# Layer one's source part by seven quarter products, one row quarter staged in pieces, and the second norm moved into layer two

## The chip, the cores and the metric

The kernel runs on one core of a Trainium2 chip. The metric is device time in microseconds (us); a comparison takes medians of several runs. TensorE (PE in the profile, PEld for its weight loads) multiplies, VectorE (DVE), ScalarE (ACT) and GpSimd (POOL) do elementwise work, and SyncE's queue (SPq) issues most DMA transfers.

## The reference, cut to what matters

For each of 16 graphs there are 1024 nodes with 128 features, `x`, and a weighted adjacency `adj` of 1024 x 1024. A first GNN is added to `x` and normalised; a second GNN of four layers, with the adjacency in both directions, is added to that and normalised again:

```python
degree = adj.sum(axis=-1)[:, :, None]
nb = einsum('bid,bij->bjd', x, adj) / degree
x = layernorm(x + relu(concat([x, nb]) @ W.T + b))

def layer(nodes):
    src_agg = einsum('bjv,bij->biv', nodes @ ws + bs, l2norm(adj, 2))   # rows normalised
    dst_agg = einsum('bjv,bji->biv', nodes @ wd + bd, l2norm(adj, 1))   # columns normalised
    self_rep = nodes @ wn + bn
    return tanh(concat([src_agg, self_rep, dst_agg]) @ wu + bu)

f1 = layer0(x); f2 = layer1(f1); f3 = layer2(concat([f2, f1]))
f4 = layer3(concat([f3, f1, x])); out = layernorm(x + f4)
```

All is in float32. The source part of a layer needs the adjacency transposed and scaled by row (`at`); the destination part needs it as it is, scaled by column (`a`).

## The kernel before, in words

One loop runs over the 16 graphs (b). For each it runs four layers, and between layer three and layer four the first GNN of the next graph (n = b + 1), whose adjacency has been loaded in the meantime. The weights `wu` are folded into the others beforehand, so that a layer is: messages (`messages`: eight node blocks times 256 columns into PSUM tiles `pt`, then VectorE adds the bias into `t`), then aggregation (`aggregate`), then tanh (`squash`).

The aggregation of a layer is a 2 x 2 block product: two halves of the features (v) by two halves of the nodes (h), with the contraction in two halves too. Where it is plain it takes 8 quarter products, four matmuls each. Winograd's form of Strassen's method takes 7: M1 to M4, Z11, Z12 and Z21, from sums of the messages (S1 to S4, made at the end of `messages`) and of the adjacency's quarters (T2 to T4 of `a`, Q2 to Q4 of `at`, made by `combine`; `combine_1` subtracts in place). The products go into six PSUM banks: Z0 and Z1 for the two node halves, and A, Bk, Ck and Dk, which share four rotating banks with the `pt` tiles. A is used for M1 and then for M3, Bk for M2, Ck for M4, Dk for the lower half of M3 (where there is one).

The matmuls are 64 columns wide, and `aggregate` issues them in pairs, one into the upper 64 partitions of PSUM (list `upper`) and one into the lower (list `lower`). One such pair is called a step below. Layers two, three and four take the seven products for both parts. Layer one of graphs 1 to 15 takes them for the destination part (DST) only, and the plain form for the source part (SRC), of which half is wanted only in the last eight steps. Layer one of graph 0 is written apart (`plain_layer`) and is not touched.

Work of the other engines is put between the steps: `events` (reads of the products, counted from the own-feature steps on) and `hooks` (by the step's number). PE, DVE, ACT and POOL run the instructions in the order of the program, which this fixes; only SyncE's order is chosen when the kernel is built, by when its transfers are expected to be ready.

The transposed adjacency `at` comes from four row quarters. Quarters 2 and 3 make `at[1]`, quarters 0 and 1 `at[0]`. Each is loaded by eight DMAs (`load_rows`), scaled by row on ACT (`scale_rows`) and transposed on VectorE (`transpose_rows`). All four are staged in parts of the old adjacency's buffer (`place`), two at a time: 2 and 3 from step 10 of layer four, 0 at step 23, 1 at step 27. The quarters 0 and 1 are transposed in layer one of the next graph, at steps 0 and 19, and the load of the adjacency after next (`load(n)`) follows the last of them.

The second norm (of the graph before) runs in layer one: `begin1` (transpose, add of the kept x, sum), `centre1`, `squares1`, `rstd1` (a power on POOL), `end1` (scaling and `store`). It works in `ys` under the tag "acc", which is also that of layer two's `e12`. Layer two runs `sums` of the next adjacency: per row block a square with its sum on ACT, a degree sum on ACT or VectorE, an add on POOL, through two buffers of the tag "sq". Layer three turns them into scale factors and scales the adjacency's columns.

Of the kernel before, what the change touches and what calls it, by code (L numbers as in the profile page):

```python
# [8 lines left out]
F32 = mybir.dt.float32  # L9
AF = mybir.ActivationFunctionType  # L10
# [13 lines left out]
def adj_resnorm_kernel(ctx: ExitStack, tc: tile.TileContext, x, adj, w0, b0, layers, out):  # L24
# [313 lines left out]
    def to_features(xs, name):  # L338

        dst = two.tile([P, N], F32, tag="xT", name=f"{name}T")  # L340
        nc.vector.transpose(dst, xs.rearrange("p k f -> p (k f)"))
        return dst
# [71 lines left out]
    def summed(name):  # L414
        return one.tile([P, K, C], F32, tag="acc", name=name)
# [30 lines left out]
    def load_rows(b, q, st, queue=nc.sync):  # L446


        v = adj[b, q * QB * C:(q + 1) * QB * C].rearrange("(k r) (h g j) -> h g r k j", r=C, h=NH, g=G)
        for g in range(G):  # L450
            for h in range(NH):
                queue.dma_start(st[g * C:(g + 1) * C, :, h * P:(h + 1) * P], v[h, g])
        return st

    def scale_rows(st, q, rinv):
        for k in range(QB):
            nc.scalar.activation(st[:, k], st[:, k], AF.Copy, scale=rinv[:, q * QB + k:q * QB + k + 1])  # L457

    def transpose_rows(st, q, at):
        h, o = divmod(q * QB * C, HW)  # L460
        for j in range(0, NB, NJ):
            nc.vector.transpose(  # L462
                at[h][:, j:j + NJ, o:o + QB * C].rearrange("p j (k c) -> p j k c", c=C),
                st.rearrange("p k (j c) -> p j k c", c=C)[:, j:j + NJ])
# [28 lines left out]
    def messages(b, l, feats, wm, between={}, with_sums=True):  # L493


        nch = CHUNKS[l]
        t = [one.tile([P, NJ, 2, 2, V], F32, tag=f"t{j}", name=f"t{l + 1}_{b}_{j}") for j in range(2)]
        for n, g in enumerate((2, 3, 0, 1)):
            pt = ps_t.tile([P, 2, 2 * P], F32, tag="pt", name=f"pt{l + 1}_{b}_{g}")
            for q in range(2):  # L500
                i = 2 * g + q
                for k, (f, c) in enumerate(feats):
                    nc.tensor.matmul(pt[:, q], f[:, i * P:(i + 1) * P], wm[:, 1 + c],  # L503
                                     start=(k == 0), stop=(k == nch - 1))
            j, o = divmod(2 * g, NJ)
            nc.vector.tensor_add(t[j][:, o:o + 2].rearrange("p k a v c -> p k (a v c)"), pt,  # L506
                                 wm[:, 0][:, None, :].to_broadcast([P, 2, 2 * P]))
            if n in between:
                between[n]()
        if not with_sums:  # L510
            return t


        s = slice(1 if l == 0 else 0, 2)
        S = {i: one.tile([P, NJ, 2, V], F32, tag=f"S{i}", name=f"S{i}_{l + 1}_{b}") for i in (2, 3, 4)}
        X = {(v, j): t[j][:, :, :, v] for v in range(2) for j in range(2)}
        S[1] = X[1, 0]
        if l == 0:
            nc.vector.tensor_sub(S[2][:, 0:2, 0], X[0, 0][:, 0:2, 0], X[1, 0][:, 0:2, 0])
        for part in (DST, SRC) if l else (DST,):  # L520
            nc.vector.tensor_sub(S[3][:, :, part], X[0, 0][:, :, part], X[1, 0][:, :, part])
        nc.vector.tensor_add(S[1][:, :, s], X[1, 0][:, :, s], X[1, 1][:, :, s])
        nc.vector.tensor_sub(S[2][:, :, s], S[1][:, :, s], X[0, 0][:, :, s])
        nc.vector.tensor_sub(S[4][:, :, s], X[0, 1][:, :, s], S[2][:, :, s])
        return X, S
# [31 lines left out]
    def aggregate(b, l, feats, msgs, a, at, T, Q, fT, etag, hooks={}, pieces=1):  # L557
# [11 lines left out]
        Dk = product(f"m3_{l}_{b}") if l else None  # L569
# [7 lines left out]

        def src(v, h, j):
            return (X[v, j // NJ][:, j % NJ, SRC], at[h][:, j])
# [30 lines left out]


        if l == 0:
            upper = [
                (Z1, True, own(1, 1)), (Z0, True, own(1, 0)),
                (Z1, False, [src(1, 1, j) for j in range(2, NB)]),
                (A, True, prod("M1", DST)), (Bk, True, prod("M2", DST)), (A, True, prod("M3", DST)),
                (Z0, False, prod("Z21", DST) + [src(1, 0, j) for j in range(NB)]),
# [3 lines left out]
                (Z1, False, [(S[2][:, j, SRC], at[1][:, j]) for j in range(2)] + [src(0, 1, j) for j in range(2, NB)]),  # L621
                (Ck, True, prod("M4", DST) + [src(1, 1, j) for j in range(2)]),
                (Z1, False, prod("Z12", DST)),
                (Z0, False, prod("Z11", DST) + [src(0, 0, j) for j in range(NB)]),
            ]
            def m4_and_m2_read():
                m4_read()
                m2_read()

            def m3_and_second_half():  # L630
                m3_read()
                second_half()

            events = {10: m1_read, 14: m4_and_m2_read, 18: m3_and_second_half}
        else:
            def m3_half():
                nc.scalar.copy(e1[high], Dk[low])

# [22 lines left out]

            def m2_and_half_of_m3():
                m2_read()
                nc.vector.tensor_add(e0[high], e0[high], e1[high])  # L664

            def last_reads():
                m3_read()
                second_half()
# [51 lines left out]
    w0n = two.tile([P, 2 * P], F32, tag="xT", name="w0n")  # L720
# [27 lines left out]
    for l, q in enumerate((2, 3, None, None)):  # L748
        fetched.append(fetch_weights(raw, l, nc.sync, None if l else wm))
        if q is not None:  # L750
            rows[q] = load_rows(0, q, places[q])
# [9 lines left out]
    xT = two.tile([P, N], F32, tag="xT", name="x0_T")  # L761
# [52 lines left out]
    x1T = two.tile([P, N], F32, tag="xT", name="x1_0_T")  # L814
# [79 lines left out]
    for q in (0, 1):  # L894
        rows[q] = load_rows(0, q, places[q], nc.gpsimd)
# [16 lines left out]
    for b in range(B):  # L912
# [4 lines left out]

# [61 lines left out]
        else:  # L979
            nm = f"1_{b - 1}"  # L980
            t = messages(b, 0, feats, wm)
            wm = message_weights(b, 1)
            w = {"ys": summed(f"y{nm}")}
            Q = combined(b, "Q")

            def begin1(w=w, nm=nm):
                transpose_rows(rows[0], 0, at)
                norm_spread(w["ys"], f4, KS)
                w["s"] = norm_sum(w["ys"], KS, nm, back)

            def scale1():
                scale_rows(rows[1], 1, rinv)

            def centre1(w=w, nm=nm):
                combine(4, y, T)
                w["sq"] = norm_centre(w["ys"], w["s"], KS, nm)

            def squares1(w=w, nm=nm):
                w["v"] = norm_squares(w["sq"], KS, nm)

            def rstd1(w=w, nm=nm):
                w["r"] = norm_rstd(w["v"], KS, nm)
                transpose_rows(rows[1], 1, at)
                if nxt:
                    w["a"] = load(n)
                    w["xs"] = load_spread(n)

            def end1(w=w):
                norm_end(w["ys"], w["r"], KS)
                store(b - 1, w["ys"], KS)  # L1010

            hooks = {0: begin1, 7: scale1, 12: centre1, 17: squares1, 19: rstd1,
                     22: lambda: combine_1(yt), 25: end1, 28: lambda: combine(2, yt, Q)}
            aggregate(b, 0, feats, t, a, at, T, Q, f1, "row", hooks)
            a2, xs2 = w.get("a"), w.get("xs")
# [7 lines left out]
        def quarters2(b=b):  # L1023
            for i in ((2, 3, 4) if b == 0 else (3, 4)):
                combine(i, yt, Q)

        hooks = {0: quarters2}
        if nxt:
            for i in ALL:
                hooks[5 + 2 * i if i < 3 else 4 + 3 * i] = lambda i=i: sums(n, a2, st, (i,))  # L1030
        if b == 0:
            hooks[12] = lambda: combine(4, y, T)
        aggregate(b, 1, feats, t, a, at, T, Q, f23, "acc", hooks)


# [43 lines left out]
        if nxt:  # L1079
# [7 lines left out]
            def add0(w=w):  # L1087
                w["ys"] = summed(f"y0_{n}")
                for h in range(NH):
                    add_x(yT, xT2, h)  # L1090
# [20 lines left out]
            def rows0():  # L1111
                for i, q in enumerate((2, 3)):
                    rows[q] = load_rows(n, q, place(i))

            def end0(w=w):
                norm_end(w["ys"], w["r"], KS)
                w["x1"] = two.tile([P, N], F32, tag="xT", name=f"x1_{n}_T")
                for h in range(NH):
                    x1_features(n, w["ys"], h, w["x1"])
                w["kept"] = put_aside(n, w["ys"])  # L1120
# [7 lines left out]
            def rows1(w=w):  # L1128
                at2[1] = transposed(n, 1)
                transpose_rows(rows[2], 2, at2)  # L1130
                scale_rows(rows[3], 3, rinv)
                w["back"] = take_back(b, kept)
                rows[0] = load_rows(n, 0, place(0))

            def rows2():
                transpose_rows(rows[3], 3, at2)
                rows[1] = load_rows(n, 1, place(1))
# [81 lines left out]
```

## Time and profile before

| | |
|---|---|
| median of three runs | 2507.22 us (2505.8 to 2507.23) |
| the profiled execution | 2505.85 us, span 2503.9 us |
| PE, PEld busy | 2484.5 us (99%), 1060.0 us (42%) |
| DVE, ACT, POOL busy | 1658.2, 836.3, 520.8 us |
| POOL power of the norms, L378 | 30 times, 5.43 us each |
| POOL add of squares, L252 | 90 times, 2.45 us each |
| row scaling, L457 | 480 times, 0.495 us each |

The span runs from the first to the last recorded instruction. A busy PE is not PE at its peak, since matmuls are pipelined and their recorded spans overlap; a length of a stage is read from the starts of its first matmuls. An L with a number is a line of the kernel before. A row of the time line has the start in us from the span's start, the length in us, engine, line, operation, output and input tiles, shape, number of merged instructions, and in brackets the idle time before it with what ended it.

### The profile page before, as it was taken

The numbers are of one execution on the slowest core, as the hardware profiler recorded it, in microseconds if no ns is written. First come the engines' busy times: TensorE is split into PE (matmuls) and PEld (weight loads), VectorE is DVE, ScalarE is ACT, GpSimd is POOL, SyncE is SP. The second block draws the span as 40 slices with busy tenths as digits, with TensorE's granted clock in tenths as the row PEclk, the third lists the DMA queues.
The fourth block names the chain that finished last, engine by engine and source line by source line (L and its number), as shares of the span: only waits on it lengthen the run. The fifth ranks groups of instructions, "written<-read, shape, count | busy, mean of one in ns | idle before, by whom it ended". The sixth has DMA issues, their size and how long they took to land.

```text
span 2503.9 us, 30302 instructions
## 1 busy us (share of the span) xinstructions
PE 2484.5 (99%) x11693; PEld 1060.0 (42%) x11693; DVE 1658.2 (66%) x2030; ACT 836.3 (33%) x1553; POOL 520.8 (21%) x217
## 2 busy tenths in 40 slices
PE   8999999999999999999999999999999999999998
PEld 4443344433444344453434434334443344433444
DVE  5858666585675757667576675766758667585643
ACT  5414333142431423324143251432414333142411
POOL 5401204112040121302113030130301203112000
PEclk9999999999999999999999999999999999999999
DMA  9418255271543615436163451635417255271410
GB/s 199 103 47 147 55 97 103 52 143 41 102 101 71 129 34 105 104 66 127 35 124 85 85 107 47 131 66 101 96 46 147 54 99 102 51 144 40 93 24 9
DMA packets 358735, 219.63 MB, mean 88 GB/s; under 512 B 148928, under 2 KB 329408, under 8 KB 358592
## 3 DMA queue, kind: packets, MB, share of 16 engines
q1 hardware_dynamic: 357184, 213.51, 42.2%
q0 software_dynamic: 1408, 4.20, 0.8%
q8 instruction: 92, 1.51, 0.3%
q14 instruction: 51, 0.42, 0.1%
HBM read 199.17 MB, written 18.46 MB: 87 GB/s over the span
## 4 chain that ended last, share of the span: by engine, by line
PE 86%; SPq 3%; DVE 2%; DMA 2%; ACT 2%; issue 2%; POOL 0%; POOLq 0%; DVEq 0%; ACTq 0%
PE m L691 34%; PE z L691 25%; PE pt L503 15%; PE pa L179 8%; SPq L231 3%; PE pw L179 2%; DMA a<-in_adj_dram 2%; DMA out_dram<-y 1%; DVE e L664 1%; ACT sq L248 0%; ACT sq L245 0%; PE d L554 0%; DVE cols L247 0%; DVE at L462 0%; POOL acc L250 0%
## 5 line engine op out<-in xcount | busy, mean ns | idle before, releaser
L378 POOL TENSOR_TENSOR rs<-ve,mhalf 128x32 f32<-128x32 f32 x30 | 162.8, 5427 | 1364.0 <-DVE ve L376 1364.0
L691 PE MATMUL m<-T,S 128*64 128x512 f32 x1008 | 395.9, 594 | 0.0
L691 PE MATMUL z<-at,t 128*64 128x512 f32 x1224 | 383.7, 592 | 0.0
L691 PE MATMUL m<-a,t 128*64 128x512 f32 x1008 | 366.8, 594 | 0.0
L691 PE MATMUL m<-Q,S 128*64 128x512 f32 x768 | 339.2, 593 | 0.0
L691 PE MATMUL m<-at,t 128*64 128x512 f32 x828 | 311.2, 592 | 0.0
L506 DVE TENSOR_TENSOR t<-pt,wm 128x512 f32<-128x512 f32 x256 | 175.4, 690 | 168.5 <-PE pt L503 168.4
L252 POOL TENSOR_TENSOR acc<-acc,sq 128x1024 f32<-128x1024 f32 x90 | 220.6, 2451 | 137.1 <-ACT sq L248 133.5
L691 PE MATMUL z<-a,S 128*64 128x512 f32 x504 | 228.3, 593 | 0.0
L691 PE MATMUL z<-a,t 128*64 128x512 f32 x504 | 226.8, 592 | 0.0
L691 PE MATMUL z<-T,t 128*64 128x512 f32 x504 | 226.8, 593 | 0.0
L336 DVE TENSOR_TENSOR a<-a,cinv 128x512 f32<-128x512 f32 x250 | 157.7, 697 | 96.3 <-DMA cinv<-dr 92.4
L457 ACT ACTIVATE a<-a,rinv 128x256 f32<-128x256 f32 x480 | 198.2, 495 | 54.9 <-DMA a<-in_adj_dram 49.5
L503 PE MATMUL pt<-wm,f1T 128*128 128x256 f32 x768 | 213.8, 384 | 0.1
L179 PE MATMUL pa<-a,xn 128*64 128x512 f32 x960 | 208.8, 592 | 0.0
L691 PE MATMUL z<-at,S 128*64 128x512 f32 x444 | 202.6, 593 | 0.0
L691 PEld LDWEIGHTS m<-Q,S 128*64 128x64 f32 x768 | 104.2, 137 | 206.6 <-issue 205.3
L591 ACT COPY e<-m 64x512 f32<-64x512 f32 x63 | 36.6, 581 | 447.8 <-PE m L691 447.5
L691 PEld LDWEIGHTS m<-T,S 128*64 128x64 f32 x1008 | 118.0, 137 | 159.6 <-issue 158.0
L691 PE MATMUL z<-Q,t 128*64 128x512 f32 x384 | 172.6, 593 | 0.0
L691 PEld LDWEIGHTS z<-at,t 128*64 128x64 f32 x1224 | 120.8, 137 | 121.0 <-issue 111.3
L691 PEld LDWEIGHTS m<-a,t 128*64 128x64 f32 x1008 | 110.1, 137 | 125.7 <-issue 120.0
(197 smaller groups left out, 3781.8 us busy)
## 6 DMA issues: line engine op xcount, KB each, us to landing
a<-in_adj_dram SPq DMA_DIRECT2D x120, 512.0 KB, 12.6
a<-in_adj_dram SPq DMA_DIRECT2D x480, 128.0 KB, 4.1
xn<-in_x_dram SPq DMA_DIRECT2D x128, 64.0 KB, 2.1
wm<-wsave SPq DMA_DIRECT2D x16, 512.0 KB, 3.9
wm<-wsave SPq DMA_DIRECT2D x31, 256.0 KB, 2.9
xs<-in_x_dram SPq DMA_DIRECT2D x60, 128.0 KB, 3.4
cinv<-dr SPq DMA_DIRECT2D x30, 256.0 KB, 5.1
dinv<-dr SPq DMA_DIRECT2D x30, 256.0 KB, 5.1
```

The source lines that it names most:

```text
L179: nc.tensor.matmul(out[s], x[:, s], y, start=start, stop=stop)
L231: nc.sync.dma_start(ov[g, :, ks], ys[g * C:(g + 1) * C, ks])
L252: nc.gpsimd.tensor_add(acc, acc, sq)
L336: engine.tensor_mul(a[:, i, s], a[:, i, s], cinv[:, s])
L378: nc.gpsimd.tensor_tensor(rstd, ve, mhalf[:, :n], ALU.pow)
L457: nc.scalar.activation(st[:, k], st[:, k], AF.Copy, scale=rinv[:, q * QB + k:q * QB + k + 1])
L503: nc.tensor.matmul(pt[:, q], f[:, i * P:(i + 1) * P], wm[:, 1 + c], start=(k == 0), stop=(k == nch - 1))
L506: nc.vector.tensor_add(t[j][:, o:o + 2].rearrange("p k a v c -> p k (a v c)"), pt, wm[:, 0][:, None, :].to_broadcast([P, 2, 2 * P]))
L591: nc.scalar.copy(e0[high], A[high])
L664: nc.vector.tensor_add(e0[high], e0[high], e1[high])
L691: nc.tensor.matmul(o, x, y, start=start, stop=stop)
```

## The change

In layer one of graphs 1 to 15 the source part is computed by the seven quarter products too. For that all of S1 to S4 are made for both parts, Dk is used, and the lists and events of layer one are new. Both row quarters of `at[0]` are transposed at step 0, T4 is made at step 3, Q2 to Q4 at steps 7, 9 and 23, and layer two no longer makes Q3 and Q4 for these graphs.

Row quarter 1 is staged in two tiles of the tag "sq" instead of the old adjacency's buffer, by 16 DMAs of half the size instead of 8; it is loaded at step 10 of layer four and scaled at step 27, before the last tanh. Quarter 0 stays where it was. The load of the next adjacency is issued at step 5 of layer one.

The second norm runs in layer two, beside the sums, with `ys` under a tag of its own ("xa"), shared with the transposed x; the transposed x1 has the tag "xb". In SyncE's queue the store of the result follows the load of the next adjacency, the weights of layer three and the load of `xs`; before, it followed the adjacency's load directly.

```diff
-        s = slice(1 if l == 0 else 0, 2)
...
-        if l == 0:
-            nc.vector.tensor_sub(S[2][:, 0:2, 0], X[0, 0][:, 0:2, 0], X[1, 0][:, 0:2, 0])
-        for part in (DST, SRC) if l else (DST,):
+        for part in (DST, SRC):
             nc.vector.tensor_sub(S[3][:, :, part], X[0, 0][:, :, part], X[1, 0][:, :, part])
-        nc.vector.tensor_add(S[1][:, :, s], X[1, 0][:, :, s], X[1, 1][:, :, s])
-        nc.vector.tensor_sub(S[2][:, :, s], S[1][:, :, s], X[0, 0][:, :, s])
-        nc.vector.tensor_sub(S[4][:, :, s], X[0, 1][:, :, s], S[2][:, :, s])
+        nc.vector.tensor_add(S[1], X[1, 0], X[1, 1])
+        nc.vector.tensor_sub(S[2], S[1], X[0, 0])
+        nc.vector.tensor_sub(S[4], X[0, 1], S[2])
...
         if l == 0:
             upper = [
                 (Z1, True, own(1, 1)), (Z0, True, own(1, 0)),
-                (Z1, False, [src(1, 1, j) for j in range(2, NB)]),
-                (A, True, prod("M1", DST)), (Bk, True, prod("M2", DST)), (A, True, prod("M3", DST)),
-                (Z0, False, prod("Z21", DST) + [src(1, 0, j) for j in range(NB)]),
+                (A, True, prod("M1", DST)), (Bk, True, prod("M2", DST)), (Z0, False, prod("Z21", DST)),
+                (A, False, prod("M1", SRC)), (Bk, False, prod("M2", SRC)), (A, True, prod("M3", SRC)),
+                (Z0, False, prod("Z21", SRC)),
             ]
             lower = [
                 (Z1, True, own(0, 1)), (Z0, True, own(0, 0)),
-                (Z1, False, [(S[2][:, j, SRC], at[1][:, j]) for j in range(2)] + [src(0, 1, j) for j in range(2, NB)]),
-                (Ck, True, prod("M4", DST) + [src(1, 1, j) for j in range(2)]),
-                (Z1, False, prod("Z12", DST)),
-                (Z0, False, prod("Z11", DST) + [src(0, 0, j) for j in range(NB)]),
+                (Dk, True, prod("M3", DST)), (Ck, True, prod("M4", DST)), (Z1, False, prod("Z12", DST)),
+                (Z0, False, prod("Z11", DST)), (Ck, False, prod("M4", SRC)), (Z1, False, prod("Z12", SRC)),
+                (Z0, False, prod("Z11", SRC)),
             ]
...
-            events = {10: m1_read, 14: m4_and_m2_read, 18: m3_and_second_half}
+                m2_and_half_of_m3()
+
+            events = {8: m3_half, 16: m1_read, 20: m4_and_m2_read, 24: last_reads}
...
-            hooks = {0: begin1, 7: scale1, 12: centre1, 17: squares1, 19: rstd1,
-                     22: lambda: combine_1(yt), 25: end1, 28: lambda: combine(2, yt, Q)}
+            def rows3():
+                for q in (1, 0):
+                    transpose_rows(rows[q], q, at)
+
+            def next_rows(w=w):
+                combine_1(yt)
                 if nxt:
                     w["a"] = load(n)
...
+            hooks = {0: rows3, 3: lambda: combine(4, y, T), 5: next_rows, 7: lambda: combine(2, yt, Q),
+                     9: lambda: combine(3, yt, Q), 23: lambda: combine(4, yt, Q)}
             aggregate(b, 0, feats, t, a, at, T, Q, f1, "row", hooks)
...
+            w = {"ys": summed(f"y{nm}", "xa")}
+            sums_of_next = {1 + 3 * i: sums_of(i) for i in ALL} if nxt else {}
...
+            hooks = {0: begin1, 11: centre1, 14: squares1, 17: rstd1, 26: end1, **sums_of_next}
         aggregate(b, 1, feats, t, a, at, T, Q, f23, "acc", hooks)
...
             def rows0():
                 for i, q in enumerate((2, 3)):
-                    rows[q] = load_rows(n, q, place(i))
+                    rows[q] = load_rows(n, q, [place(i)])
+                rows[1] = load_rows(n, 1, [two.tile([P, QB // 2, NH * P], F32, tag="sq", name=f"rows1_{n}_{i}")
+                                           for i in range(2)])
...
-                rows[0] = load_rows(n, 0, place(0))
+                rows[0] = load_rows(n, 0, [place(0)])
 
             def rows2():
                 transpose_rows(rows[3], 3, at2)
-                rows[1] = load_rows(n, 1, place(1))
+                scale_rows(rows[1], 1, rinv)
```

## The prediction

> **What bounds the kernel now.** I read the page's busy times first, then the windows of one batch (batch 4: layer one with its messages, layer two, layer three with the first GNN of the next batch, layer four), then the time lines of TensorE and VectorE inside them.
>
> ```profile
> PE 2484.5 (99%) x11693; PEld 1060.0 (42%) x11693; DVE 1658.2 (66%) x2030; ACT 836.3 (33%) x1553; POOL 520.8 (21%) x217
> 515.03:546.53 31.50, 31.50 (x154) 12.31 (x152) 26.68 (x29) 12.66 (x25) 5.48 (x2) 1.00 0.66 115
> 546.53:576.08 29.55, 29.55 (x138) 11.53 (x136) 20.43 (x19) 16.14 (x28) 12.51 (x5) 1.00 0.62 121
> 576.08:628.78 52.70, 52.39 (x250) 21.01 (x248) 30.58 (x49) 9.79 (x16) 7.63 (x3) 1.00 0.14 41
> 628.78:668.91 40.13, 40.13 (x194) 18.97 (x193) 26.59 (x30) 13.20 (x26) 5.43 (x1) 1.00 0.50 107
> ```
>
> The columns are the stretch, its length, busy time of PE, PEld, DVE, ACT and POOL, granted clock, DMA share, GB/s. PE never rests at full clock, so work taken from PE shortens the kernel, and any late operand lengthens it at once. But layer one, the stage that is edited, has VectorE busy 26.7 of its 31.5 us: the average of 66% hides that. Now TensorE there, and VectorE there and in layer two:
>
> ```profile
> 518.68 1.94 PE L691 MATMUL z<-x_T,wown 128*64 128x512 f32 x8
> 520.45 0.59 PE L691 MATMUL z<-at,t 128*64 128x512 f32 x1
> ...
> 527.32 1.89 PE L691 MATMUL m<-a,t 128*64 128x512 f32 x8
> ```
>
> A step is a pair of matmuls, four records. Step 0 starts at 518.68, step 2 at 520.45, step 10 at 527.32: (527.32 - 520.45) / 8 = 0.859 us a step.
>
> ```profile
> 518.79 0.69 DVE L506 TENSOR_TENSOR t<-pt,wm 128x512 f32<-128x512 f32 x1 [0.17 <-PE pt L503]
> ...
> 521.62 2.37 DVE L462 STREAM_TRANSPOSE at<-a 128x1024 f32<-128x1024 f32 x2 [0.23 <-ACT a L457]
> ...
> 527.55 2.28 DVE L489 TENSOR_TENSOR T<-a,T 128x2048 f32<-128x2048 f32 x1
> ```
>
> VectorE is released by the last message at 518.79, never earlier. T4 (L489) is made from 527.55 and needed only much later, in the last DST group.
>
> ```profile
> 550.29 0.69 DVE L506 TENSOR_TENSOR t<-pt,wm 128x512 f32<-128x512 f32 x1 [0.17 <-PE pt L503]
> 551.02 0.76 DVE L521 TENSOR_TENSOR S<-t 128x256 f32<-128x256 f32 x2
> 551.81 0.69 DVE L522 TENSOR_TENSOR t<-t,t 128x512 f32<-128x512 f32 x1
> 552.54 0.69 DVE L523 TENSOR_TENSOR S<-t 128x512 f32<-128x512 f32 x1
> 553.26 0.69 DVE L524 TENSOR_TENSOR S<-t,S 128x512 f32<-128x512 f32 x1
> 553.87 2.28 DVE L487 TENSOR_TENSOR Q<-Q,at 128x2048 f32<-128x2048 f32 x1
> 556.07 4.45 DVE L489 TENSOR_TENSOR Q<-at,Q 128x2048 f32<-128x2048 f32 x1
> ```
>
> This is the full set of sums as the changed layer one will have it: from step 0 of layer two (550.18) to the next instruction, 3.69 us. The last line, 4.45 for 2.28, stands beside a POOL add (555.64 to 558.38).
>
> [...] the two-input L664 takes 0.69 us alone and 2.59 beside a POOL add, while the one-input L247 stays at 1.22; beside the power of L378 nothing is stretched.
>
> **Removed.** For 15 batches the source part of layer one costs 28 matmuls for 32: 30 steps for 32. 2 x 0.859 = 1.72 us a batch, 25.8 us in all. Certain: it is a count.
>
> **First wait: T4 at step 10.** The new order puts Z21's destination part (T4) at step 10, which is 1.77 + 8 x 0.859 = 8.64 us after step 0. VectorE must first do, in its order: the sums, until 3.69; four transposes of 128x512 for the quarter in two pieces (L418's same shape is 0.69 recorded, 0.65 from start to start), 2.60; two of 128x1024, 2.37; then T4, 2.28. End 10.94; about 0.07 until PE moves. Wait 2.37 us. Behind it stand Z12 of the same step and all later matmuls. Bounds: with transposes at 0.60 and nothing for the signal 2.1, at 0.69 2.6. The rows themselves are not late: the quarter in row one is scaled before the last tanh of layer four (ACT is idle there), that of row zero by about 521.6 as now, and its transposes begin only at about 525.
>
> **Next: Q4 at step 26.** After T4 VectorE does at1 - at0, Q2 and Q3, 3 x 2.28, until 17.8; Q2 is needed at step 18 (17.9 with the first wait) and Q3 at 22 (21.3), so both are just in time. Q4 stands behind the reading of M2, which is ready at step 22. That chain stands in layer three:
>
> ```profile
> 608.67 0.69 DVE L599 TENSOR_TENSOR e<-e,m 64x512 f32<-64x512 f32 x1
> 609.39 0.62 ACT L600 COPY e<-e 64x512 f32<-64x512 f32 x1 [10.34 <-DVE e L599]
> 610.04 0.69 DVE L664 TENSOR_TENSOR e<-e,e 64x512 f32<-64x512 f32 x1 [0.68 <-ACT e L600]
> ```
>
> From step 22: 0.27 until the product is seen, two ACT copies of M4 (1.17), the L600 copy (0.62), then L664 until 2.75, then Q4 until 5.0. Step 26 comes 3.43 after step 22. Wait 1.65 us with the signal; 1.1 if the copy did not stand behind M4's two. Layer one in sum: -1.72 + 2.37 + 1.65 = +2.30 us.
>
> **Moved to layer two: the norm, beside the sums of the next adjacency.** Per batch VectorE gains there a transpose, add, reduce, centring, squares and scaling (6 x 1.22) and loses Q3 and Q4. Two small PE groups (0.09 each) move with it. Counted from the first message: the squares of row block 0 start at 1.6 (the load was issued some 10 us earlier than now, so no longer the bound), 2.3 us each on ACT; POOL's first add ends at 9.0; the norm's two-input add runs to 12.1, its reduce to 13.25, just at step 11 (13.13): 0.2 late. ACT reaches the norm's square only after M1's and M3's copies and block 3, at 16.65; its reduce ends at 18.95; the power's input is wanted at step 17, 18.6 with the small groups: 0.45 late. With the signals I take 0.75 us, bounds 0 and 1.2. On POOL adds 2 to 5 (2.36 each) run behind these squares until 25.1, then the power (5.43) until 30.5. Only then the norm's scaling L383 (1.22), in front of the last e0 add and the tanh that layer three's messages want 3.9 after they start (30.3). [...] L383 ends at 34.1, tanh at 35.5, and PE waits 1.3; if VectorE is first, tanh ends at 33.2 and a wait of 0.33 us that layer three has now (52.45 mean against 52.12 best) may go. So +1.0 or -0.3; I take the middle, +0.35.
>
> **DMA and queues.** Rows one costs 16 issues of 0.45 us on SP for 8 of 0.51, seven of them ahead of rows two and three; they leave from 486.6 to 489.8 and those are released only at 492.8. Now rows zero, 8 issues, runs alone at 509.5 and lands no later than at 518.3. The store (18.09 us of SP queue behind the 4 MB load) comes after the load, and with it the ACT wait on it (22.3 us, off the path) goes; its buffer is wanted 14 us later. The new weight and xn loads behind it have 5 us to spare. Nothing for these edits; if the store again took 18 us, the transpose into its buffer would be some 4 us late, with 3 us of cover before the GNN.
>
> **Sum.** 15 x 2.30 + 14 x 0.75 + 14 x 0.35 = 34.5 + 10.5 + 4.9 = 49.9 us (the last batch has no sums). The profiled execution took 2505.85 (span 2503.9, 1.95 around it); it becomes 2555.8. The median, 2507.22, is 1.4 above: **2557 us**.
>
> **Rivals.** *Layer two absorbs everything*: POOL's chain has slack, the 0.33 goes: 34.5 - 4.6 = +30, 2537. For it: ACT is busy 16.1 of 29.6 there. Against: it runs in lockstep with POOL. *Only one wait in layer one* (say Q4 hidden): -1.72 + 2.37 = +0.65, +10, 2517; nothing in the rows speaks for it. *The other side*: T4 in time and Q4 hidden, -25.8, 2481. It decides if T4 starts within 6.3 us of step 0 instead of 8.66; that needs the six transposes in 2.6 us instead of 4.97, against every row of L462. *The norm becomes the bound of layer three*: [...] 2 us more a batch, 2585. That the quarter products aren't run is no rival: the listed PE instructions have them.
>
> **How the numbers follow.** Both waits with something in layers two and three 0.60; absorbed 0.20; one wait 0.07; other side 0.08; worse than 2582 0.05. Range 2525 to 2582: the first two with the bounds (2.1 and 1.1 instead of 2.37 and 1.65 take off 12 us). About 0.2% is what a measurement of this kernel can tell from no change. Slower 0.89, same 0.03, faster 0.08.
>
> **What would show it.** Layer one with messages 33.8 us for 31.5; PE idle about 2.4 us before the first Z21 matmul of T and 1.6 before that of Q, released by VectorE; small waits at the norm's two groups in layer two; ACT's wait on the store gone. Layer one at 29.8 would prove me wrong; layer two above 31 or layer three above 54 would mean the norm costs more.

## The result and the profile after

The changed kernel takes 2603.88 us (median of four runs, 2603.05 to 2604.17) where the kernel before takes 2507.22: a ratio of 1.0381, with a 95% interval of 1.0365 to 1.0396. The profiled execution took 2603.05 us with a span of 2601.0, which is 97.1 more than the span of before.

The first view is the page's busy times. An L is now a line of the changed kernel: the aggregation's matmuls are L688, the messages' L510, and every `combine` is L496.

```profile
PE 2497.5 (96%) x11573; PEld 1046.9 (40%) x11573; DVE 1721.1 (66%) x2075; ACT 841.5 (32%) x1568; POOL 532.6 (20%) x217
```

The x behind a number counts records. The 120 PE records that are missing (11693 before) are the removed work: 4 matmuls of 2 records in 15 graphs. So PE has less to do, and yet shows 13 us more busy time, at 96% of a longer span for 99%. Less work that takes longer points to waits and to the clock. The list of PE's waits shows the waits; its columns are the sum in us, the number of waits and the longest.

```profile
PE pt L510 <- ACT f23T L701: 32.2, 28, 2.1
PE z L688 <- DVE T L496: 27.7, 15, 1.9
PE z L688 <- DVE Q L496: 23.2, 15, 1.5
PE pv L179 <- DVE v L368: 2.8, 14, 0.2
```

Before, the first of them read as in the next line, and the others were not there:

```profile
PE pt L503 <- ACT f23T L704: 1.3, 4, 0.4
```

The lower three of the changed kernel are the waits the prediction named in layer one and layer two. The first is in layer three. The windows of graph 4 (layer one with its messages, layer two, layer three with the next first GNN, layer four, then two short stretches of layer three) show what each stage lost and where the clock went:

```profile
689.02:722.40 33.38, 29.99 (x138) 11.32 (x136) 25.72 (x27) 10.50 (x22) 0.00 (x0) 1.00 0.70 139
722.40:752.70 30.30, 30.09 (x146) 11.56 (x144) 22.91 (x24) 18.24 (x31) 16.46 (x6) 1.00 0.17 33
752.70:809.33 56.63, 54.34 (x250) 22.15 (x248) 32.90 (x49) 8.74 (x14) 10.34 (x4) 0.97 0.21 47
809.33:849.46 40.13, 40.13 (x195) 18.95 (x193) 26.58 (x30) 14.67 (x30) 5.48 (x2) 1.00 0.65 132
757.16:759.41 2.25, 0.17 (x1) 0.00 (x0) 2.25 (x4) 0.72 (x1) 2.25 (x1) 1.00 0.19 30
759.41:762.93 3.52, 3.52 (x9) 2.86 (x10) 3.04 (x4) 0.00 (x0) 0.80 (x1) 0.52 0.85 130
```

Over the graphs the stages take 33.39, 30.30, 56.62 and 40.12 us, for 31.50, 29.55, 52.45 and 40.12 before: +1.89, +0.75, +4.17 and nothing. The sum is 15 x 1.89 + 14 x 0.75 + 14 x 4.17, with +0.24 for the last graph's layer two and -0.46 for graph 0: 97.0 us. The last two rows are the core of it. PE loses 2.25 us before the third group of layer three's messages, and then the granted clock is 0.52 for the next 3.5 us. The clock's own records say that it is halved for exactly 3.413 us, from 759.44. It happens once in each of graphs 1 to 14; in the kernel before it happens in none. Half of 3.413, 1.71 us, is what each such stretch can cost a PE that is busy all through it.

Layer one, on the time line:

```profile
696.36 2.48 DVE L469 STREAM_TRANSPOSE at<-rows 128x512 f32<-128x512 f32 x4
698.76 2.33 DVE L469 STREAM_TRANSPOSE at<-a 128x1024 f32<-128x1024 f32 x2
701.01 2.25 DVE L496 TENSOR_TENSOR T<-a,T 128x2048 f32<-128x2048 f32 x1
703.32 0.64 PE L688 MATMUL z<-T,t 128*64 128x512 f32 x1 [1.84 <-DVE T L496]
715.75 0.69 DVE L617 TENSOR_TENSOR e<-e,e 64x512 f32<-64x512 f32 x1 [1.12 <-ACT e L601]
716.47 2.29 DVE L496 TENSOR_TENSOR Q<-at,Q 128x2048 f32<-128x2048 f32 x1
718.82 0.64 PE L688 MATMUL z<-Q,t 128*64 128x512 f32 x1 [1.55 <-DVE Q L496]
```

Both predicted waits are there, released by the predicted instructions: T4 behind the six transposes, Q4 behind the reading of M2. Against the normal spacing of the steps they cost 2.01 and 1.71 us (the brackets give the idle time alone, 1.84 and 1.55).

The end of layer two and the start of layer three:

```profile
745.17 1.06 ACT L248 ACTIVATE sq<-a 128x1024 f32<-128x1024 f32 x1 [1.28 <-POOL acc L252]
746.40 2.36 POOL L252 TENSOR_TENSOR acc<-acc,sq 128x1024 f32<-128x1024 f32 x1 [1.26 <-ACT sq L248]
748.71 5.90 POOL L378 TENSOR_TENSOR rs<-ve,mhalf 128x32 f32<-128x32 f32 x1
753.61 0.70 PE L510 MATMUL pt<-wm,f23T 128*128 128x256 f32 x2 [0.20 <-ACT f23T L701]
754.58 5.63 POOL L252 TENSOR_TENSOR acc<-acc,sq 128x1024 f32<-128x1024 f32 x2
754.64 3.37 DVE L383 TENSOR_TENSOR y<-y,rs 128x1024 f32<-128x1024 f32 x1 [0.71 <-POOL rs L378]
757.93 0.68 DVE L690 TENSOR_TENSOR e<-e,z 128x512 f32<-128x512 f32 x1
758.03 2.66 SPq L231 DMA_DIRECT2D out_dram<-y  x4
758.64 0.72 ACT L701 ACTIVATE f23T<-e,bout 128x512 f32<-128x512 f32 x1 [4.04 <-DVE e L690]
759.41 1.22 PE L510 MATMUL pt<-wm,f23T 128*128 128x256 f32 x2 [2.09 <-ACT f23T L701]
763.36 0.59 PE L510 MATMUL pt<-wm,f1T 128*128 128x256 f32 x2
```

Read it from the bottom. The third group waits for the tanh L701; the tanh for the last addition of e0, L690; that stands on VectorE behind the scaling of the second norm, L383; and L383 waits for the power, L378, which came to POOL 26.3 us after layer two began. POOL's next additions start at 754.58, just ahead of L383, which is recorded with 3.37 us for 1.22. Then two matmuls take 1.22 us where the last row's two take 0.59: the half clock.

In the kernel before, no instruction of the second norm stands in this place. There layer three starts at 576.08, and the addition (L693) and the tanh (L704) begin 2.4 and 3.1 us later, where they now begin 5.2 and 5.9 us after it:

```profile
578.46 0.68 DVE L693 TENSOR_TENSOR e<-e,z 128x512 f32<-128x512 f32 x1
579.17 0.72 ACT L704 ACTIVATE f23T<-e,bout 128x512 f32<-128x512 f32 x1
```

### The profile page after: what moved, and what is told of

The parts are those of the page before. It is cut to its first block, busy times and chain, and to the rows that moved or that the text cites. A ratio compares the mean times of both kernels' runs of the same rounds, so it can differ in the third digit from the quotient of the medians.

```text
span 2601.0 us, 30284 instructions
## 1 busy us (share of the span) xinstructions
PE 2497.5 (96%) x11573; PEld 1046.9 (40%) x11573; DVE 1721.1 (66%) x2075; ACT 841.5 (32%) x1568; POOL 532.6 (20%) x217
## 4 chain that ended last, share of the span: by engine, by line
PE 76%; DVE 7%; POOL 7%; ACT 4%; issue 3%; DMA 2%; SPq 0%; DVEq 0%; ACTq 0%; POOLq 0%
PE m L688 30%; PE z L688 20%; PE pt L510 14%; PE pa L179 8%; POOL acc L252 4%; POOL rs L378 3%; DVE at L469 2%; PE pw L179 2%; ACT sq L248 1%; DVE Q L496 1%; DVE T L496 1%; DMA wm<-wsave 1%; DMA a<-in_adj_dram 1%; ACT sq L245 1%; PE pa L796 1%
## 5 line engine op out<-in xcount | busy, mean ns | idle before, releaser
L688 PE MATMUL m<-Q,S 128*64 128x512 f32 x1008 | 447.4, 593 | 0.0
L688 PE MATMUL m<-T,S 128*64 128x512 f32 x1008 | 396.4, 593 | 0.0
L688 PE MATMUL m<-at,t 128*64 128x512 f32 x1008 | 391.2, 592 | 0.0
L688 PE MATMUL m<-a,t 128*64 128x512 f32 x1008 | 390.5, 593 | 0.0
L378 POOL TENSOR_TENSOR rs<-ve,mhalf 128x32 f32<-128x32 f32 x30 | 169.3, 5645 | 889.8 <-DVE ve L376 889.8
L688 PE MATMUL z<-T,t 128*64 128x512 f32 x504 | 227.5, 594 | 27.7 <-DVE T L496 27.7
L688 PE MATMUL z<-Q,t 128*64 128x512 f32 x504 | 227.3, 594 | 23.2 <-DVE Q L496 23.2
L688 PEld LDWEIGHTS m<-Q,S 128*64 128x64 f32 x1008 | 135.8, 137 | 270.7 <-issue 270.4
L688 PE MATMUL z<-at,S 128*64 128x512 f32 x504 | 231.1, 594 | 0.0
L688 PE MATMUL z<-a,S 128*64 128x512 f32 x504 | 227.3, 594 | 0.0
L688 PE MATMUL z<-at,t 128*64 128x512 f32 x504 | 227.3, 594 | 0.0
L688 PE MATMUL z<-a,t 128*64 128x512 f32 x504 | 226.8, 592 | 0.0
L510 PE MATMUL pt<-wm,f1T 128*128 128x256 f32 x768 | 225.1, 400 | 0.1
L250 POOL TENSOR_TENSOR acc<-sq,sq 128x1024 f32<-128x1024 f32 x15 | 42.1, 2805 | 820.8 <-ACT sq L248 820.8
L510 PE MATMUL pt<-wm,f23T 128*128 128x256 f32 x512 | 169.0, 414 | 32.2 <-ACT f23T L701 32.2
L688 PEld LDWEIGHTS m<-at,t 128*64 128x64 f32 x1008 | 120.2, 137 | 143.9 <-issue 143.9
L688 PEld LDWEIGHTS m<-T,S 128*64 128x64 f32 x1008 | 118.9, 137 | 135.4 <-issue 135.4
```

Source lines behind the costliest of these rows:

```text
L250: nc.gpsimd.tensor_add(acc, state["sq"], sq)
L378: nc.gpsimd.tensor_tensor(rstd, ve, mhalf[:, :n], ALU.pow)
L688: nc.tensor.matmul(o, x, y, start=start, stop=stop)
```

## Experiments

The theory after the result (the first one in the expectations) has three causes. In layer three, `end1` stands ahead of the last e0 addition, and the wait that it makes also halves TensorE's clock for 3.413 us after it. In layer one, T4 comes too late for step 10. And Q4 comes too late for step 26. The rivals are that layer three's loss is another late operand or a clock that falls for other reasons (the load on the chip, the new order of layer one), and that the quarter products of layer one are a loss in themselves; what each would give for a kernel stands in its expectation.

The table has the stages of all kernels in us, as means over graphs 1 to 14. Its last column counts the stretches of half clock inside the graphs, in the profiled execution of each kernel. The kernel before, run beside each group of experiments, took 2506.2 to 2507.6 us, so differences of the medians below some 1.5 us are not read.

| kernel | median | layer one | two | three | four | half clock |
|---|---|---|---|---|---|---|
| before | 2507.22 | 31.50 | 29.55 | 52.45 | 40.12 | 0 |
| changed | 2603.88 | 33.39 | 30.30 | 56.62 | 40.12 | 14 |
| e1: `end1` after the last e0 | 2557.28 | 33.39 | 30.30 | 53.30 | 40.12 | 0 |
| e2: two matmuls in the wait | 2579.73 | 33.39 | 30.30 | 54.95 | 40.12 | 0 |
| e3: T4 before the transposes | 2554.74 | 31.32 | 30.30 | 54.95, 3 of 14: 56.57 | 40.12 | 3 |
| e4: Q4 earlier | 2554.88 | 31.62 | 30.30 | 54.96 | 40.12 | 0 |
| e5: e1, e3 and e4 | 2498.86 | 29.55 | 30.30 | 53.29 | 40.12 | 0 |
| e6: no second norm | 2530.04 | 33.39 | 29.55 | 52.12 | 40.12 | 0 |
| e7: e5, sums first | 2490.70 | 29.55 | 29.88 | 53.12 | 40.12 | 0 |
| e8: e7, power last | 2477.32 | 29.55 | 29.88 | 52.12 | 40.12 | 0 |
| e9: two matmuls in layer four | 2606.09 | 33.39 | 30.30 | 54.95, 1 of 14: 56.64 | 41.84 | 1 |

### e1: the norm's end behind the last e0 addition

```diff
-            hooks = {0: begin1, 11: centre1, 14: squares1, 17: rstd1, 26: end1, **sums_of_next}
+            hooks = {0: begin1, 11: centre1, 14: squares1, 17: rstd1, **sums_of_next}
         aggregate(b, 1, feats, t, a, at, T, Q, f23, "acc", hooks)
         if b:
+            end1()
```

> The changed kernel with the norm's scaling (end1) called after layer two's last e0 add instead of at step 26. Theory 1, the wait and the half clock behind it are one chain [...]: both vanish in layer three, 2.25 + 1.71 us a batch, less up to 0.8 us that the message adds behind the scaling then cost: 3.2 to 4.0 us in 14 batches, 2604 to 2548-2559. Theory 2, the half clock has a cause of its own: only the wait goes, 2.25 us, 2572.

2557.28 us (2555.97 to 2557.64), 1.0198 [1.0183, 1.0214] of before. Half of the loss is gone with one call moved. In PE's waits the row that had 28 waits keeps only the short one at the start of the messages, in layer three:

```profile
PE pt L510 <- ACT f23T L701: 2.9, 14, 0.2
```

Layer three falls by 3.3 us a graph, more than the 2.25 of the wait, and no graph has a stretch of half clock. So `end1` is the late operand. What remains above 52.12 is 0.48 at the start of the messages, and 0.70 at the start of the aggregation: the time line has VectorE's transpose of POOL's sum (L261) waiting 1.05 us for POOL, the message sums behind it, and the first matmul on such a sum at 912.78, 0.71 after its partner of the same step (912.07).

### e2: work put into the wait

Two matmuls into a tile that nobody reads are put before the third group of layer three's messages. Nothing that was late comes earlier.

```diff
+            if n == 2 and fill:
+                pf = small(f"fill{l}_{b}", [HW])
+                for _ in range(fill):
+                    nc.tensor.matmul(pf, wm[:, 1, :P], feats[0][0][:, :HW], start=True, stop=True)
```

> The changed kernel with two matmuls of 128x128 by 128x512 that nothing reads (about 0.86 us each) in front of the third message group of layer three, where TensorE waits 2.25 us. Theory 1, the idle time brings the clock down: the wait is nearly filled, the clock stays whole, 1.7 us a batch go, 2580, though two matmuls were added. Theory 2, the clock goes down for another reason: 2604 or more.

2579.73 us (2579.11 to 2580.41), 1.0289 [1.0274, 1.0304]. With more work for PE the kernel is 24.2 us faster than the changed one, 14 x 1.72. The time line of PE (lines are 4 further on in this kernel):

```profile
910.26 1.88 PE L509 MATMUL fill<-f1T,wm 128*128 128x512 f32 x4
912.95 0.70 PE L514 MATMUL pt<-wm,f23T 128*128 128x256 f32 x2 [0.38 <-ACT f23T L705]
913.49 0.60 PE L514 MATMUL pt<-wm,f1T 128*128 128x256 f32 x2
```

The third group still waits for the tanh, 0.38 us after the filling, but its two matmuls take 0.70 us (1.22 in the changed kernel) and the next 0.60, and none of the 14 graphs has a stretch of half clock. So the half clock is a consequence of PE's idleness, not of the new order or the load, and it costs 1.7 us a graph by itself. (The added matmuls also move what follows by 1.7 us; that this is not what kept the clock whole is read from the same trace under e9.)

### e3 and e4: one wait of layer one each

e3 makes T4 before the six transposes. e4 makes Q4 at step 11, right after Q3, instead of behind M2's reading at 23.

```diff
+            def t4_and_rows3(y=y, T=T):
+                combine(4, y, T)
+                rows3()
...
-            hooks = {0: rows3, 3: lambda: combine(4, y, T), 5: next_rows, 7: lambda: combine(2, yt, Q),
+            hooks = {0: t4_and_rows3, 5: next_rows, 7: lambda: combine(2, yt, Q),
```

> The changed kernel with T4 made at step 0 of layer one before the transposes of the rows. T4 is then ready 6.0 us after step 0, 2.6 before it is wanted, at0 at 10.8 of 12.1, Q2 at 15.3 of 15.5. Theory of the two waits: the first goes, 2.0 us in 15 batches, 2574; the second stays. If the first wait only moves on to Q2 or Q3: 2604 to 2590.

```diff
-                     9: lambda: combine(3, yt, Q), 23: lambda: combine(4, yt, Q)}
+                     9: lambda: combine(3, yt, Q), 11: lambda: combine(4, yt, Q)}
```

> The changed kernel with Q4 made at step 11 of layer one, after Q3, instead of step 23 behind the reading of M2. Theory of the two waits: the second goes, 1.7 us in 15 batches, 2578. If the wait at step 26 were for the message sums or for the reads themselves: 2604.

e3 took 2554.74 us (1.0188 [1.0173, 1.0203]), e4 2554.88 (1.0191 [1.0174, 1.0208]). Each removes its own wait and leaves the other: layer one is 2.07 shorter in e3 and 1.77 in e4, within 0.06 of the 2.01 and 1.71. But both kernels are some 20 us faster than expected, though nothing in layer three was edited. PE's waits, e3 first and e4 second:

```profile
PE pt L510 <- ACT f23T L701: 32.1, 28, 2.1
PE z L688 <- DVE Q L496: 23.2, 15, 1.5
```

```profile
PE pt L510 <- ACT f23T L701: 32.1, 28, 2.1
PE z L688 <- DVE T L496: 27.7, 15, 1.9
```

The wait of layer three is the same as in the changed kernel: 28 times, 2.1 at most. Yet the clock was halved after it in 3 graphs of 14 in e3 and in none in e4. (That is the profiled execution; in two of e4's four the mean clock was 0.997 instead of 0.999 and the span some 3 us longer, so there it may have been halved once or twice.) Two windows of layer three of e3:

```profile
898.17:953.13 54.96, 52.65 (x250) 20.84 (x248) 32.74 (x49) 8.74 (x14) 10.36 (x4) 1.00 0.21 49
1524.95:1581.52 56.57, 54.29 (x251) 22.11 (x249) 32.89 (x49) 8.74 (x14) 10.33 (x4) 0.97 0.21 48
```

The same work and the same wait take 54.96 us with the clock at 1.00 and 56.57 at 0.97. So a second condition beside the wait decides. The clock's own records have a candidate. In the changed kernel the 14 halved stretches are 3.413 us long and begin 160.43 us apart, which is 47.0 of that length. The one before them, at 39.23 us, and the one at the kernel's end, at 2599.23, begin 70.0 and 69.0 lengths from their neighbours; in the kernel before, the only two begin 721.0 lengths apart. So in the records of both kernels the clock falls on a grid of 3.413 us, and in the changed kernel the wait falls at the same place of that grid in every graph. In e4 the graph's period is 157.00 us, 46.0 intervals of the grid: again nearly the same place every time, but one where the wait crosses the edge of two intervals. In e3 the period of a graph with full clock is 156.69, 45.9 intervals, so the place moves on by 0.3 us a graph and is hit now and then.

### e9: the same wait, another place on the grid

That was tested on the changed kernel by putting the two matmuls of e2 into the messages of layer four of graphs 1 to 14, where nothing waits. They make each graph longer by 1.7 us and leave layer three as it is. A window in the expectation is an interval of the grid.

```diff
-        t = messages(b, 3, feats, wm, between)
+        t = messages(b, 3, feats, wm, between, fill=2 if b and nxt else 0)
```

> The changed kernel with two matmuls more (0.86 us each, read by nothing) in the messages of layer four in graphs 1 to 14, 1.71 us a graph, far from the wait in layer three. Theory, the clock is halved only where the 2.04 us wait falls into one window of a grid of 3.413 us: the added time moves the wait by half a window, all but the first graph keep the full clock, 14 x 1.71 - 13 x 1.71, so 2604 to 2607 in spite of 24 us of matmuls more. Rival, the half clock follows each such wait wherever it falls: 2628.

2606.09 us (2604.93 to 2606.32), 1.0397 [1.0382, 1.0413]. The 28 matmuls cost layer four 14 x 1.71 = 24 us, and the kernel only 2.2 over the changed one. In graph 1 the clock was halved as before (the wait is still at its old place, and the halved stretch begins at 280.27); in the other thirteen it was not. The wait of graph 5 and what follows:

```profile
920.62:922.87 2.25, 0.15 (x1) 0.00 (x1) 2.25 (x4) 0.72 (x1) 2.25 (x1) 1.00 0.19 31
922.87:926.39 3.52, 3.52 (x16) 2.77 (x18) 3.04 (x4) 0.00 (x0) 0.80 (x1) 1.00 0.86 129
```

The wait is as long as at 757.16 in the changed kernel, but 16 matmul records fit into the 3.52 us behind it where 9 did. In 188 intervals of 3.4133 us (160.43 / 47) from 280.27, an edge lies at 921.98, so some 1.2 us of the idle time fell into one interval and 0.9 into the next. A graph at full clock takes 160.47 us here, again 47.0 intervals, so the wait stays near the place to which that one loss had moved it. The place on the grid is shown as the second condition, for these waits.

The same count can be made for every such wait in the changed kernel, e3, e4 and e9, with the edges taken from the clock's records in each trace. There are 56 such waits, of 2.08 to 2.10 us each. In 18 of them at least 2.02 us lay in one interval, and the clock was halved behind each; in the other 38 at most 1.73 us did, and it was halved behind none. e2 can be read again with this. Its clock records put an edge at 910.23 and the next at 913.64, and without the filling, which starts at 910.26, PE would have been idle from some 910.4 to 912.5. That lies wholly in one interval, as it does in 7 of the 14 graphs of e2, and still the clock stayed whole. So it was the filling that kept it, not a change of place.

### e5: the three repairs together

> The changed kernel with the three moves at once: T4 before the transposes, Q4 after Q3, the norm's scaling after layer two's last e0 add. If the waits add up: layer one with messages 33.4 - 2.1 - 1.8 = 29.5 us, layer two 30.3, layer three 53.3 as in the run with that move alone, no half clock: 0.35 us a batch below the kernel before, 2500. If the VectorE chain of layer one becomes too long for Q2, Q3 and Q4 together: 2510 to 2530.

2498.86 us (2498.26 to 2499.78), 0.9968 [0.9955, 0.998] of before. With both waits of layer one gone, that layer takes 29.55 us: 31.50 less two steps (1.72) and less two small groups of the norm that went to layer two. Each of these costs 0.12 in the kernel before: 0.09 until the next pair starts, and 0.03 because that pair is slower. So the quarter products do save what they remove. The gain is eaten by layers two (+0.75) and three (+0.84).

### e6: no second norm in layer two

```diff
-            hooks = {0: begin1, 11: centre1, 14: squares1, 17: rstd1, 26: end1, **sums_of_next}
+            hooks = {0: spread_only, 11: load_next, 26: store_only, **sums_of_next}
```

> The changed kernel with the second norm left out of layer two for graphs 0 to 14: their outputs are the transposed fourth features alone, stored without adding x and without normalising. The waits of layer one stay. If the norm's place makes the losses of layers two and three: layer two 29.5, layer three 52.2, full clock, about 4.9 us a batch, 2535. If the earlier sums and the new DMA order make them: 2600 still.

2530.04 us (2529.6 to 2530.62), 1.0092 [1.0078, 1.0106]. The windows of layers two and three:

```profile
863.18:892.73 29.55, 29.55 (x138) 11.51 (x136) 19.68 (x20) 18.92 (x33) 15.20 (x7) 1.00 0.16 32
892.73:944.86 52.13, 52.13 (x251) 21.09 (x249) 28.22 (x46) 6.98 (x11) 4.99 (x2) 1.00 0.15 42
```

PE is busy for the whole of both. So the wider edit of layer one costs 15 x 1.89 = 28 us, and the norm in layer two the other 73.8 us (2603.88 - 2530.04; by stages 14 x (0.75 + 4.50) = 73.5). Against the kernel before that is 69 us, because layer three had lost 0.33 a graph there, which is gone in e6. Since e6 has no second norm at all, it shows what the norm's presence in layer two costs, not that every place there costs as much.

### e7 and e8: the order on POOL

e7 is e5 with the sums of the next adjacency moved and `end1` at step 0 of layer three, behind the sums of the messages. e8 also asks for the power at step 26, so that POOL has it behind the last addition.

```diff
-            sums_of_next = {1 + 3 * i: sums_of(i) for i in ALL} if nxt else {}
+            sums_of_next = {k: sums_of(i) for i, k in enumerate((1, 4, 7, 12, 13, 18, 24, 25))} if nxt else {}
...
-        hooks, between = {}, {}
+        hooks, between = {0: end1} if b else {}, {}
```

> As the run with the three moves, but the scaling and the store at step 0 of layer three behind the message sums, the squares of row block 3 after the norm's centring, those of block 5 after the reading of M2, and those of blocks 6 and 7 after the tanh. If the rest of the losses are VectorE's and ACT's order: layer two 29.7, layer three 52.2, 151.6 us a batch, 2477. If POOL's adds end too late for the transpose of their sum, layer three stays near 53.3: 2493.

```diff
-            hooks = {0: begin1, 11: centre1, 14: squares1, 17: rstd1, **sums_of_next}
+            hooks = {0: begin1, 11: centre1, 14: squares1, 26: rstd1, **sums_of_next}
```

> As the reordered run at 2491, with the norm's power (and what feeds it) at step 26 instead of 17, so that POOL takes it after the last add of squares. If the 0.9 us that layer three still loses are POOL's power in front of the adds: layer three 52.2, layer two 29.7, 2476. If something else makes the sums late: layer three stays at 53.1, 2491.

e7 took 2490.70 us (0.9934 [0.9918, 0.9949]), the second of its two expected values. VectorE's transpose of POOL's sum, in e7 and then in e8:

```profile
886.68 1.25 DVE L261 STREAM_TRANSPOSE acct<-acc 128x1024 f32<-128x1024 f32 x1 [2.94 <-POOL acc L252]
```

```profile
880.39 1.25 DVE L261 STREAM_TRANSPOSE acct<-acc 128x1024 f32<-128x1024 f32 x1 [0.80 <-POOL acc L252]
```

In e7 the power stands ahead of POOL's last three additions and makes them late for VectorE, which holds up the sums of layer three behind that transpose. In e8 the wait is 0.80, and nothing of it reaches PE:

```profile
815.71:845.26 29.55, 29.55 (x138) 11.46 (x137) 25.62 (x27) 10.50 (x22) 0.00 (x0) 1.00 0.57 122
845.26:875.14 29.88, 29.88 (x146) 11.64 (x145) 22.25 (x24) 18.55 (x31) 12.53 (x5) 1.00 0.40 73
875.14:927.26 52.12, 52.12 (x250) 21.08 (x248) 30.19 (x49) 8.30 (x15) 13.00 (x4) 1.00 0.22 51
927.26:967.39 40.13, 40.13 (x195) 18.95 (x193) 26.58 (x30) 14.66 (x30) 5.47 (x2) 1.00 0.62 133
```

PE is busy for the whole of all four stages. 2477.32 us (2476.46 to 2477.7), 0.9883 [0.9867, 0.99] of before: the same change, ordered otherwise, is 1.2% faster than before and 4.9% faster than as it was made.

## Why the prediction was wrong

The direction was right and the time was not: 2557 predicted with a range to 2582, 2603.88 measured. Step by step, against its own sums:

- **Removed: right.** 30 steps for 32, 120 PE records fewer, and e5's layer one shows the 1.72 us. The sum forgot that two small groups of the norm leave layer one, 0.24 us with the slower pairs behind them.
- **First wait, T4: mechanism right, size 2.01 for 2.37.** The transposes took 2.40 and 2.25 us for 2.60 and 2.37, so T4 started 8.34 us after step 0 (at 692.67), not 8.66. e3 confirms the cause.
- **Next, Q4: right**, 1.71 for 1.65. e4 confirms that M2's reading held it. Layer one in sum came to +1.89 for +2.30, 28 us for 34.5: -1.72 - 0.24 + 2.07 + 1.77 = +1.88, with the waits as e3 and e4 take them away.
- **Layer two: the waits are the named ones, the equal number (0.75 for 0.75) is in part luck.** The two groups came 0.08 and 0.42 us late, for 0.2 and 0.45 with something for the signals. The other 0.24 is the groups' own time, which the sum had left out here as it had in layer one.
- **The failed step is the end of "Moved to layer two"**, the wait of layer three's messages for the tanh. It weighed an order in which L383 comes behind POOL's next addition (+1.0) against one in which it comes first (-0.3), and took +0.35 as the middle. It measured +4.17, 58 us for 4.9. That splits into 0.48 - 0.33 + 2.25 + 1.71 = 4.11:
  - The worse order came in every graph, and its wait was 2.25 us, not 1.3. POOL's additions and ACT's squares waited for each other in turn (1.26 and 1.28 in the rows above) instead of following at 2.36. So the power began 26.3 us after layer two's start for 25.1, and then took 5.90 for 5.43. The tanh ended at 36.96 for 35.5, and the group that wants it came at 34.76 for 34.2.
  - The 0.33 that layer three already lost did not go but became 0.48.
  - The clock was halved behind the wait, 1.71 us. The clock was in no step and in no rival: a wait was priced by its length alone.
- **L383 and POOL's next addition: as in the worse of the two orders.** The addition began first (754.58, L383 at 754.64), and L383 is recorded with 3.37 us beside it for 1.22. In e8, where POOL records nothing beside it (from 885.75 to 888.89), L383 takes 1.22 (at 886.97). What makes it longer beside an addition was not shown.
- **DMA and queues: right that nothing comes of them.** The store takes 2.66 us of SP's queue for 18.09, ACT no longer waits for it, and no wait of PE for the new loads is in its list. The 16 issues of row quarter 1 took 10.5 us in all (7 in 3.53, 9 in 6.99) for 7.2, without effect.
- **Rivals.** "The norm becomes the bound of layer three" (2585; all above 2582 was given 0.05) was the nearest and names the right place: its 2 us a batch fit the wait of 2.25, and without the half clock e2 took 2579.73. Its sign, layer three above 54, came. The upper end of the range has no full working: the bounds that are named add up to 2576, not 2582. "The other side" (2481) needed both waits of layer one gone; with that alone the kernel would still have been short of it, as e5 shows. It took e8's order as well.

## What to carry to other kernels

A norm, or any chain that ends in another engine's slow instruction, belongs behind the operands that TensorE wants next, on every queue that it passes: here one call (`end1`) in front of the last addition cost 47 us. When PE has been busy without a gap, price a new gap not only by its length: ask whether the clock can fall behind it (here 1.71 us a graph behind 2.09 us of idle time), and if a gap can't be removed, harmless matmuls in it may cost less than nothing (e2: 24.2 us less). When two orders are possible and one is far worse, the middle of both is the forecast of neither.

## What the runs showed of the hardware

- **A wait of some 2 us can halve TensorE's clock.** In the changed kernel the idle time was 2.09 us, and the clock fell to half for 3.413 us, in 14 graphs of 14. What decided was how much of the wait lay in one interval of the grid of 3.413 us on which the falls begin: 2.02 us or more in all 18 cases where it fell (least in e3, where the matmul came 0.08 us behind the edge at 2316.64), 1.73 or less in the 38 where it did not. The T4 waits of layer one, 1.85 us idle, never did it in any run, also in the 62 of 90 that lay wholly in one interval. What the limit is between 1.85 and 2.02, whether it is one of idle time alone, and what makes the grid, stays open.
- **The loss keeps itself in step.** With the clock full a graph of the changed kernel would take 158.72 us, 46.5 intervals; the 1.71 us lost to the clock make it 160.43, 47.0 intervals, and so the next graph's wait meets the same place again. That is why it happened every time, and why an unrelated edit of 1.7 us (e3, e4, e9) changed the time by some 20 us beyond its own worth.
